# Four graph layers on one core: SyncE's transfers ordered by the framework instead of by the written plan

## The chip, the cores and the metric

The kernel runs on one core of a Trainium2 chip. The metric is device time in microseconds (us). The kernel before took 3899.66 us, the median of three runs (3894.99 to 3900.15). The profile shown here is of one further execution, which took 3905.45 us and has a span of 3903.3 us.

## The reference

The input is 64 graphs of 256 nodes with 512 features each, a 256x256 adjacency matrix for each graph, and the weights of four layers. All is float32. Every layer has the same frame, and the four layers differ in what they do with the normalised features:

```python
h = jnp.maximum(_layernorm(x, axis=-1), 0.0)
x = x + _L0_gnn_ref(h, adj, L0_gnn_W_qk, L0_gnn_W_v)      # scores q k^T * adj, summed, softmax over nodes, times v
...
x = x + _L1_gnn_ref(h, adj, ...)                          # 8 heads, leaky relu of e_i + e_j, masked softmax, times feats
...
x = x + _L2_gnn_ref(h, adj, ...)                          # 8 heads, tanh(adj * Xc Xp^T) times Xp
...
x = x + _L3_gnn_ref(h, adj, nodemask, L3_gnn_Wqk, L3_gnn_Wv)  # q * (adj @ k), softmax over nodes, times v
```

The graphs are independent of each other. Within a graph the four layers follow each other.

## The kernel before

One graph is one chain of 140 named steps (the function `graph`, from L621). Its tiles are 128 partitions (half of the nodes) by 512 features. About five graphs are in work at a time, each in another layer, so that TensorE always finds matmuls of some graph.

**The plan.** Every step has a due time, written out by hand in a table: `TIMES` for the graphs in the middle, which repeat with `PERIOD` = 60.2, and the tables `FIRST` and `LAST` for the graphs at the two ends. `Plan.sequence` (L364) sorts the steps of all graphs by these times, and `Plan.run` (L372) traces them in that order. After each step, `run` ties every new instruction to the one traced before it on the same engine, for the engines listed in `PINNED` (L35). Those engines therefore execute in the order of the due times. The framework, Tile, adds the semaphores, and for an engine that is not tied it chooses the order itself, from its own estimate of when each instruction can start.

**Buffers.** `keep` (L439) makes each kind of buffer once, in a fixed number: five `xt` (a graph's features), three `adj`, two `blocks`, five `at`, two `hn`, three `ht`, two `sq`, three `all`, eight PSUM banks. A step takes the buffer that has been free longest and gives it back with `done`; this bookkeeping happens in the order of tracing, so who gets which buffer is fixed by the plan and does not depend on the order of an engine.

**The transfers.** All 2,747 transfers are issued by SyncE (SP in the profile). For each graph of the steady middle they are, by step:

- `load` (L627): the features `xt` (L629), the adjacency matrix `adj` (L630), and the same matrix once more in 32-wide `blocks`, as four transfers of 64 KB (L634). VectorE turns `blocks` into the transposed matrix `at` (L639); GpSimd turns `adj` into an additive mask in place (L644).
- `sw0` to `sw3`, `swx`, `swy` (L700): VectorE transposes 32x32 squares into `sq`, and this writes them (512 KB) to DRAM as `sq_d`.
- `ht0` to `ht3`, `xpt` (L618): `sq_d` is read back in four transfers, which completes the transpose; TensorE multiplies with `ht` at L607 and with `xpt` at L994. `yr` (L1076) does the same for layer 2's output, and GpSimd and VectorE add it to `xt` at L1083.
- In layer 1: `er` (L835) writes the heads' scores to DRAM, `enes` reads them back to all partitions in two transfers of 1 MB (L839 for the neighbours' scores, L840 for a node's own). VectorE takes the masked maximum of them at L852, then `mr` (L884) writes the maxima and `mb` (L888) reads them back to all partitions, 1 MB. VectorE subtracts them at L910 (step `eb`), ScalarE takes the exponential at L916 (`ex`), and TensorE multiplies at L928 (`po`).
- `store` (L1134): the finished `xt` to the output.

The weights are loaded in the same way among the first graphs' steps (L488 to L560).

Tile gives these transfers eight semaphores in turn, and a transfer waits on SP's queue until the one that had its semaphore before has landed, besides waiting for what it reads and for its buffer.

Of the kernel before, what the change touches and what calls it, by code (L numbers as in the profile page):

```python
# [18 lines left out]
KC = D // P  # L19
# [12 lines left out]
NEG_BIG = -1e10  # L32
BIG = 3.0e38

PINNED = (mybir.EngineType.PE, mybir.EngineType.Activation, mybir.EngineType.DVE, mybir.EngineType.Pool, mybir.EngineType.SP,)  # L35

PERIOD = 60.2
TIMES = {
# [312 lines left out]
class Plan:  # L351
# [20 lines left out]
    def run(self, weights, graph, count):  # L372
        graphs = {-1: weights()}
        for _, b, name in self.sequence(count):
# [5 lines left out]
            for i in traced[n:]:  # L380
                if i.engine in PINNED:
                    if i.engine in self.last:
# [5 lines left out]
class Graph:  # L388
# [5 lines left out]
    def step(self, name):  # L394
        def add(run):
            self.steps[name] = run
            return run
        return add
# [19 lines left out]
def tile_four_gnn_layers(ctx: ExitStack, tc: tile.TileContext, x, adj, nodemask,  # L418
# [5 lines left out]
    nc = tc.nc  # L424
# [14 lines left out]
    def keep(kind, count, shape, pool=None):  # L439

        plan.pools[kind] = [(pool or held).tile(shape, F32, name=f"{kind}{i}") for i in range(count)]
# [35 lines left out]
    def weights():  # L477

        g = Graph(plan)
        step = g.step  # L480
        st = {}


        def plain(name, t, src):
            @step(name)
            def _():
                for r in range(4):
                    nc.sync.dma_start(t[r::4], src.rearrange("(k r d) e -> r d k e", k=KC, r=4)[r])  # L488

        def by_heads(name, k, t, src):  # L490
            @step(f"{name}{k}")
            def _():
                for r in range(4):
                    first = k * P + r * S
                    nc.sync.dma_start(t[r::4].rearrange("p (h u) -> p h u", h=H),
                                        src[:, first:first + S, :].rearrange("h d u -> d h u"))

        def to_all(name, t, src):
            @step(name)
            def _():  # L500
                nc.sync.dma_start(t, src.rearrange("h u -> (h u)").partition_broadcast(P))
        plain("wqk", wqk0_s, wqk0)
        plain("wv0", wv0_s, wv0)
        plain("wv3", wv3_s, wv3)
        for k in range(KC):
            by_heads("w1", k, w1_s[:, k, E:], w1)
            by_heads("w2", k, w2_s[:, k], w2)
        to_all("b1", b1_bc, b1)
        to_all("b2", b2_bc, b2)


        @step("c2")
        def _():
            for s in range(2):
                half = slice(s * U, (s + 1) * U)
                nc.sync.dma_start(c2_s[half, :, half], c2t.rearrange("(a s) k j -> s k a j", s=2)[s])


        @step("wa")
        def _():  # L520
            st["a"] = once.tile([P, 2, D], F32, name="a_bc", bufs=1)
            for s, a in enumerate((a_self, a_neigh)):
                nc.sync.dma_start(st["a"][:, s], a.rearrange("h u -> (h u)").partition_broadcast(P))

        def times_a(k):
            @step(f"sa{k}")
            def _():
                for s in range(2):
                    prod = once.tile([P, D], F32, name="prod", bufs=1)
                    nc.vector.tensor_mul(prod, w1_s[:, k, E:], st["a"][:, s])  # L530
                    nc.vector.tensor_reduce(w1_s[:, k, s * H:(s + 1) * H], prod.rearrange("p (h u) -> p h u", h=H),
                                            AX.X, OP.add)
        for k in range(KC):
            times_a(k)


        @step("mk")
        def _():
            st["mask"] = once.tile([B, N], F32, name="mask_rows", bufs=1)
            nc.sync.dma_start(st["mask"], nodemask)  # L540

        @step("mkp")
        def _():
            pm = g.take("bank", name="mask")
            for c in range(NC):
                nc.tensor.transpose(pm[:, c * B:(c + 1) * B], st["mask"][:, c * P:(c + 1) * P], ident[:B, :B])

        @step("mkv")
        def _():
            nc.vector.tensor_copy(mask_c, g["mask"][:, :NC * B].rearrange("p (c b) -> p c b", c=NC))  # L550
            g.done("mask")


        def part_of_m(e):
            @step(f"wn{e}")
            def _():
                st[f"wn{e}"] = w_n = once.tile([P, 2, KC, P], F32, name="w_n")
                for s in range(2):
                    first = s * D + e * P
                    nc.sync.dma_start(w_n[:, s], wqk3[:, first:first + P].rearrange("(k p) e -> p k e", p=P))  # L560

            @step(f"mt{e}")
            def _():
                for s in range(2):
                    pt = g.take("bank", name=f"wt{s}")
                    for k in range(KC):
                        nc.tensor.transpose(pt[:, k * P:(k + 1) * P], st[f"wn{e}"][:, s, k], ident)

            @step(f"mv{e}")
            def _():  # L570
                st["w_t"] = w_t = once.tile([P, 2, D], F32, name="w_t", bufs=1)
                nc.vector.tensor_copy(w_t[:, 0, :].rearrange("p (k d r) -> p k d r", k=KC, r=4),
                                      g["wt0"].rearrange("p (k r d) -> p k d r", k=KC, r=4))
                nc.vector.tensor_copy(w_t[:, 1, :], g["wt1"])
                g.done("wt0")
                g.done("wt1")

            @step(f"mm{e}")
            def _():
                for k in range(KC):  # L580
                    pm = g[f"m{k}"] if e else g.take("bank", name=f"m{k}")
                    nc.tensor.matmul(pm, st["w_t"][:, 0, k * P:(k + 1) * P], st["w_t"][:, 1, :],
                                     start=(e == 0), stop=(e == KC - 1))
        for e in range(KC):
            part_of_m(e)

        @step("ma")
        def _():
            for k in range(KC):
                nc.scalar.activation(m3_s[:, k, :], g[f"m{k}"], AF.Copy, scale=1.0 / math.sqrt(D))  # L590
                g.done(f"m{k}")


        @step("room")
        def _():
            setup.close()
            late = ctx.enter_context(tc.tile_pool(name="late", bufs=1, side="right"))
            keep("xp", 2, [P, NC, D], late)
            keep("xpt", 2, [P, HP, N], late)
            keep("xc", 1, [P, HP, N], late)  # L600
        return g
# [567 lines left out]
```

## Time and profile before

| What | Value |
|---|---|
| Median of the three runs | 3899.66 us |
| Span of the profiled execution | 3903.3 us |
| TensorE matmuls (PE) | 3811.1 us busy, 98% of the span, 17,474 instructions |
| TensorE weight loads (PEld) | 2375.3 us busy, 61% |
| VectorE (DVE) | 3033.7 us busy, 78% |
| ScalarE (ACT) | 1704.9 us busy, 44% |
| GpSimd (POOL) | 1264.8 us busy, 32% |
| DMA | 717.62 MB, mean 184 GB/s; SP's queue 74.7% of 16 engines' span |

PE and PEld are two rows of one engine: weight loads overlap the matmuls. SP has no busy time in the table, because issuing a transfer does not count as busy. In the timeline of SP each row is an issue: its start is the moment at which everything it waits for has come, and its length is the time that SP was held by the issue itself, not by the transfer. The profile has no landing times for the transfers. When one landed is seen only where some engine waited for it.

### The profile page before, as it was taken

What the parts mean: (1) busy time and instruction counts of PE and PEld (TensorE: products, weight loads), DVE (VectorE), ACT (ScalarE), POOL (GpSimd) and SP (SyncE); (2) the same over time, 40 slices, a digit from 0 to 9 for tenths busy, and PEclk for the clock granted to TensorE, in tenths of its full rate; (3) what the DMA queues carried; (4) which work ended last, traced back from release to release, by engine and by line L of the source; (5) the groups of instructions that cost most, each with busy time, mean ns of one, the idle gap of its engine ahead of it and who ended that gap; (6) DMA issues with size and microseconds to landing.
All of it is one profiled execution on the core that took longest, in us unless ns stands there. A gap on an engine that the chain in (4) does not pass through costs nothing.

```text
span 3903.3 us, 53632 instructions
## 1 busy us (share of the span) xinstructions
PE 3811.1 (98%) x17474; PEld 2375.3 (61%) x17474; DVE 3033.7 (78%) x7641; ACT 1704.9 (44%) x3333; POOL 1264.8 (32%) x1098
## 2 busy tenths in 40 slices
PE   7999999999999999999999999999999999999989
PEld 4756566566566666666666666666566665665564
DVE  6887778777877877877777788788788778777774
ACT  2444444444444444444444444444444444444342
POOL 1332323323323323323323333333233233233231
PEclk9999999999999999999999999999999999999989
DMA  8666777777777788777777877777778777777754
GB/s 211 174 189 172 179 194 174 196 193 179 194 189 184 194 185 189 192 185 181 190 186 186 196 182 187 191 181 191 191 176 200 187 181 192 187 179 193 172 145 107
DMA packets 1657607, 717.62 MB, mean 184 GB/s; under 512 B 1493936, under 2 KB 1549296, under 8 KB 1632752
## 3 DMA queue, kind: packets, MB, share of 16 engines
q1 hardware_dynamic: 1657328, 714.19, 74.7%
q8 instruction: 140, 2.29, 0.3%
q14 instruction: 139, 1.14, 0.1%
HBM read 477.56 MB, written 236.45 MB: 183 GB/s over the span
## 4 chain that ended last, share of the span: by engine, by line
PE 74%; DVE 7%; DMA 4%; SPq 2%; issue 1%; POOL 1%; ACT 1%; DVEq 0%; POOLq 0%; ACTq 0%
PE bank L607 44%; PE bank L928 10%; PE bank L1016 6%; PE bank L1030 5%; PE bank L1102 5%; PE bank L994 3%; DVE junk L852 2%; DVE sq L613 1%; DMA hn<-sq_d 1%; SPq L618 1%; DMA ht<-sq_d 1%; DVE shift L673 1%; PE bank L768 1%; PE bank L718 1%; DVE stats L657 1%
## 5 line engine op out<-in xcount | busy, mean ns | idle before, releaser
L607 PE MATMUL bank<-w_s,ht 128*128 128x256 f32 (+2 forms) x3072 | 963.4, 464 | 30.6 <-DMA ht<-sq_d 24.5
L607 PE MATMUL bank<-wv_s,ht 128*128 128x512 f32 x2048 | 914.4, 594 | 0.1
L607 PEld LDWEIGHTS bank<-w_s,ht 128*128 128x128 f32 x3072 | 572.9, 192 | 364.4 <-issue 215.6
L607 PEld LDWEIGHTS bank<-wv_s,ht 128*128 128x128 f32 x2048 | 380.8, 191 | 426.2 <-issue 410.8
L904 POOL TENSOR_TENSOR pair<-pair,negt 128x1024 f32<-128x1024 f32 x256 | 600.5, 2367 | 50.6 <-ACT pair L897 46.4
L680 ACT ACTIVATE hn<-xt,shift,rstd 128x512 f32<-128x512 f32 x512 | 388.7, 806 | 448.6 <-DVE shift L673 430.3
L928 PEld LDWEIGHTS bank<-feats,pair 128*128 128x128 f32 x4096 | 485.0, 194 | 47.9 <-issue 25.5
L897 ACT ACTIVATE pair<-all,ec 128x256 f32<-128x256 f32 x1024 | 417.2, 494 | 200.1 <-DMA all<-er_d 196.3
L928 PE MATMUL bank<-feats,pair 128*128 128x65 f32 x4096 | 480.8, 276 | 10.2 <-ACT pair L916 10.2
L1055 ACT ACTIVATE pair<-pair 128x512 f32<-128x512 f32 x512 | 294.8, 623 | 420.6 <-DVE pair L1048 420.2
L852 DVE CUSTOM_DVE_ANT_0 junk<-all,adj 128x256 f32<-128x256 f32 x1024 | 444.0, 434 | 35.2 <-DMA all<-er_d 2.1
L607 PE MATMUL bank<-m_s,ht 128*128 128x512 f32 x1024 | 465.9, 599 | 1.3 <-DVE pair L1048 0.8
L668 POOL TENSOR_TENSOR rstd<-rstd,power 128x2 f32<-128x2 f32 x256 | 180.6, 706 | 813.4 <-DVE rstd L664 804.9
L1048 DVE TENSOR_TENSOR pair<-bank,at 128x512 f32<-128x512 f32 x512 | 327.4, 683 | 107.7 <-PE bank L1016 107.0
L1083 POOL TENSOR_TENSOR xt<-xt,hn 128x512 f32<-128x512 f32 x64 | 111.5, 1742 | 924.6 <-DMA hn<-sq_d 657.9
L613 DVE STREAM_TRANSPOSE sq<-hn 128x512 f32<-128x512 f32 x512 | 337.7, 690 | 58.9 <-ACT hn L680 58.9
L657 DVE BATCH_NORM_STATS2 stats<-xt 128x6 f32<-128x512 f32 x512 | 327.2, 680 | 36.4 <-POOL xt L1083 28.6
L910 DVE TENSOR_TENSOR pair<-pair,all 128x1024 f32<-128x1024 f32 x256 | 325.9, 1292 | 9.9 <-DMA all<-m_d 7.5
L607 PEld LDWEIGHTS bank<-m_s,ht 128*128 128x128 f32 x1024 | 189.2, 190 | 213.5 <-issue 207.1
L953 POOL TENSOR_TENSOR xt<-xt,o 128x256 f32<-128x256 f32 x256 | 181.2, 729 | 386.6 <-DVE rs L941 225.1
L916 ACT ACTIVATE pair<-pair 128x1024 f32<-128x1024 f32 x256 | 262.2, 1047 | 45.1 <-DVE pair L910 39.6
L1016 PE MATMUL bank<-xc,xpt 64*128 64x256 f32 x2048 | 255.8, 389 | 1.8 <-ACT xc L1002 1.0
(77 smaller groups left out, 3866.9 us busy)
## 6 DMA issues: line engine op xcount, KB each, us to landing
sq_d<-sq SPq DMA_DIRECT2D x384, 512.0 KB
ht<-sq_d SPq DMA_DIRECT2D x1024, 128.0 KB
all<-er_d SPq DMA_DIRECT2D x128, 1024.0 KB
all<-m_d SPq DMA_DIRECT2D x64, 1024.0 KB
xt<-in_x_dram SPq DMA_DIRECT2D x64, 512.0 KB
xpt<-sq_d SPq DMA_DIRECT2D x256, 128.0 KB
hn<-sq_d SPq DMA_DIRECT2D x256, 128.0 KB
out_dram<-xt SPq DMA_DIRECT2D x64, 512.0 KB
```

Of the source, the lines that this page charges most:

```text
L607: nc.tensor.matmul(p, ht[:, k, c * P:(c + 1) * P], w[:, k], start=(k == 0), stop=(k == KC - 1))
L613: nc.vector.transpose(sq.rearrange("p (r k c i) -> p c k r i", r=4, k=KC, c=NC)[:, c], t[:, c])
L657: nc.vector.bn_stats(stats[:, c, :], g["xt"][:, c, :])
L680: nc.scalar.activation(hn[:, c, :], g["xt"][:, c, :], AF.Relu, bias=st["shift"][:, c:c + 1], scale=st["rstd"][:, c:c + 1])
L852: nc.vector.tensor_tensor_reduce(junk, g["en"][:, h, :], g["adj"][:, c, :], 1.0, -BIG, OP.add, OP.max, st["mx"][:, c, h:h + 1])
L897: nc.scalar.activation(e[:, s, j, :], g["es"][:, h, :], AF.Prelu, bias=st["ec"][:, j, H + h:H + h + 1], alpha=0.2)
L904: nc.gpsimd.tensor_tensor(e, e, g["negt"][:, None].to_broadcast([P, 2, NC, N]), OP.add)
L910: nc.vector.tensor_tensor(e, e, g["m"][:, 2 * p:2 * p + 2, None, :].to_broadcast([P, 2, NC, N]), OP.subtract)
L928: nc.tensor.matmul(po[:, h % 4, :], e[:, s, j, i * P:(i + 1) * P], feats[:, j, h, :], start=(j == 0), stop=(j == NC - 1))
L1016: nc.tensor.matmul(ps[s][:, m, :], g["xpt"][half, p, m * P:(m + 1) * P], g["xc"][half, p, :], start=True, stop=True)
L1048: nc.vector.tensor_tensor(th[:, s], g[f"ps{p}{s}"].rearrange("p (m n) -> p m n", m=NC), g["at"], OP.mult)
L1055: nc.scalar.activation(g[f"th{p}"][:, s], g[f"th{p}"][:, s], AF.Tanh)
```

## The change

`PINNED` loses SyncE. PE, ScalarE, VectorE and GpSimd stay tied to the order of the due times; SyncE's instructions are no longer tied to each other, and Tile orders them. The second part gives the four passes that transpose the last layer's weights (`part_of_m`, once per `e`) separate names for their banks in the plan's bookkeeping. It changes no instruction.

```diff
-PINNED = (mybir.EngineType.PE, mybir.EngineType.Activation, mybir.EngineType.DVE, mybir.EngineType.Pool, mybir.EngineType.SP,)
+PINNED = (mybir.EngineType.PE, mybir.EngineType.Activation, mybir.EngineType.DVE, mybir.EngineType.Pool,)
...
-                    pt = g.take("bank", name=f"wt{s}")
+                    pt = g.take("bank", name=f"wt{s}{e}")
...
-                                      g["wt0"].rearrange("p (k r d) -> p k d r", k=KC, r=4))
-                nc.vector.tensor_copy(w_t[:, 1, :], g["wt1"])
-                g.done("wt0")
-                g.done("wt1")
+                                      g[f"wt0{e}"].rearrange("p (k r d) -> p k d r", k=KC, r=4))
+                nc.vector.tensor_copy(w_t[:, 1, :], g[f"wt1{e}"])
+                g.done(f"wt0{e}")
+                g.done(f"wt1{e}")
```

Set side by side, the instruction lists of PE, DVE, ACT and POOL of the two programs are the same, row by row. The lists of SP hold the same 2,747 transfers in another order. In the steady middle, with b the graph being loaded, the two orders of one period are:

```
before: ... x(b) adj(b) blocks(b) 1-4, er, sw2, en, es, swy, ht2, sw0, yr, ht0, mr,
        mb, swx, sw3, xpt, ht3, sw1, store, ht1, x(b+1) ...
after:  ... x(b), er, sw2, en, es, swy, ht2, sw0, yr, ht0, mr, adj(b+2) blocks(b+2) 1,
        mb, swx, sw3, blocks(b+2) 2, xpt, ht3, blocks(b+2) 3-4, sw1, store, ht1, x(b+1) ...
```

Among the first eleven and the last six graphs more transfers change places.

## The prediction, made before the changed kernel ran

> **What bounds the kernel now.** I read the page's busy table first, then the busy times by stage, then the waits of PE by stage, and last the timeline of SP where the change moves transfers. The page:
>
> ```profile
> PE 3811.1 (98%) x17474; PEld 2375.3 (61%) x17474; DVE 3033.7 (78%) x7641; ACT 1704.9 (44%) x3333; POOL 1264.8 (32%) x1098
> ```
>
> The stages: for each stretch, busy us of PE, PEld, DVE, ACT and POOL (instructions in brackets), the granted clock, the DMA engines' share and GB/s:
>
> ```profile
> 0.00:250.00 250.00, 212.48 (x947) 140.58 (x947) 189.05 (x471) 93.67 (x184) 74.11 (x71) 0.95 0.76 196
> 250.00:500.00 250.00, 241.15 (x1112) 147.10 (x1111) 189.16 (x470) 108.69 (x210) 81.29 (x71) 0.99 0.69 173
> 500.00:3500.00 3000.00, 2980.50 (x13788) 1861.92 (x13787) 2380.90 (x6043) 1348.82 (x2645) 1001.39 (x863) 1.00 0.77 188
> 3500.00:3903.00 403.00, 377.01 (x1634) 225.74 (x1633) 274.56 (x659) 153.72 (x297) 107.96 (x94) 0.97 0.62 153
> ```
>
> PE sets the pace. Outside its matmuls the span holds 92 us: 37.5 in the first 250 us, 8.9 in the next 250, 19.5 in the 3,000 us of the steady middle, 26 at the end. The change touches no instruction of PE, so it can only shrink or widen these gaps. In the middle, PE's waits (us in total, times, longest) are:
>
> ```profile
> PE bank L607 <- DMA ht<-sq_d: 10.1, 11, 1.7
> PE bank L607 <- DVE mx L867: 4.0, 5, 1.0
> PE bank L718 <- DVE junk L776: 3.9, 9, 0.6
> ```
>
> Only the first is a wait for a transfer, so SP's order could win 10 us there and no more.
>
> [...] So whatever stands behind a waiting transfer on SP waits too. The trace agrees: `mr` and `mb` below start 2.49 us apart though the issue of `mr` lasts 0.30. [...]
>
> **The steady middle: cost about 0.** Per graph the change moves five issues, `adj` and four of `blocks`, while `x` stays: 0.47 us for `adj` and 0.63 for each of `blocks` (the medians of the answers on L630 and L634), 3.0 us of SP in all. They leave the place after `x`, and go into three holes of this timeline (start, length, issue):
>
> ```profile
> 1937.89 3.24 SPq L618 DMA_DIRECT2D ht<-sq_d  x4
> 1941.44 0.30 SPq L884 DMA_DIRECT2D m_d<-mr  x1
> 1943.93 0.35 SPq L888 DMA_DIRECT2D all<-m_d  x1
> 1950.90 1.50 SPq L700 DMA_DIRECT2D sq_d<-sq  x2
> 1953.58 2.88 SPq L618 DMA_DIRECT2D xpt<-sq_d  x4
> 1956.56 3.22 SPq L618 DMA_DIRECT2D ht<-sq_d  x4
> 1963.78 0.33 SPq L700 DMA_DIRECT2D sq_d<-sq  x1
> ```
>
> Hole 1, between `mr` and `mb`, is 2.19 us of waiting for `mr` to land; `adj` and one of `blocks` need 1.10. Hole 2, between `sw3` and `xpt`, is 1.18 us; one of `blocks` needs 0.63. Hole 3, between `ht3` and `sw1`, is 4.0 us; two need 1.26. So SP issues everything else when it did. None of the moved loads waits for a buffer there: `adj`(b+2) takes the buffer of the graph whose `mr` has just gone, `blocks`(b+2) one whose transpose is done.
>
> On the wire, the nearest price is the stretch 1910.8 to 1916.0, in which `x`, `adj` and `blocks`, 1 MB, took 5.2 us; `adj` and one of `blocks`, 320 KB, is then 1.6 us, a further one 0.3 (an estimate by bytes)[...]. Behind hole 1 stands `mb`: issued at 1943.93, its first reader L910 started at 1952.37 without a wait, while the DMA engines were at 5% from 1948.0 on. It has some 4 us to spare, and in the whole middle DVE waits for `mb` nowhere. Behind hole 3 stand `sw1` and `ht1`; the DMA share is 0.01 at 1962 to 1963 and 0.00 in the next us, so the two blocks land in idle time. What the loads leave is no gain: after `x` the next work is `er`, at 1921.96, and the DMA share from 1916.0 to 1921.9 is 0.12. DVE waits for `blocks` 1.2 us in the whole run, POOL for `adj` 8.8, both at the start. Bounds: -3 us (some of the `ht` waits), +10 (0.2 us per graph through `mb` or `xpt` in graphs with less room). I take 0.
>
> **The first 250 us: cost about 5.5.** Here the new order differs in what waits. Two places matter.
>
> A and B, layer 1's `ht` of the third and fifth graph. SP before:
>
> ```profile
> 115.72 2.73 SPq L618 DMA_DIRECT2D ht<-sq_d  x4
> 118.56 0.64 SPq L884 DMA_DIRECT2D m_d<-mr  x1
> 121.89 0.34 SPq L700 DMA_DIRECT2D sq_d<-sq  x1
> ```
>
> The new order puts `mr` and that `sq_d` write ahead of the four reads. The write waits for DVE's transposes until 121.89 (SP had been free since 119.2), so the reads are issued from 122.3, the last at 124.3. The nearest landing seen is that of `yr`: last issue near 1936.5, its reader released at 1940.96, 4.4 us. PE wants this `ht` at 125.99, without a gap; it would get it near 128.5: 2.5 us. At B an `adj` load for the sixth graph stands ahead of `ht`, and waits for the buffer that DVE's L852 frees at 154.3; `ht`'s last issue goes from 153.2 to 157.6, landing near 162, against PE at 158.89 plus the 2.5: 0.5 more. Between 150 and 226 PE has gaps of 0.65, 0.74, 1.22, 0.61 and 3.32 us behind DVE, ACT and DMA, which swallow lateness as far as those engines are not late themselves. Bounds 0 and 3; I take 1.
>
> C, the two 1 MB reads of the fifth graph's scores. Before:
>
> ```profile
> 223.41 0.33 SPq L700 DMA_DIRECT2D sq_d<-sq  x1
> 225.94 0.30 SPq L884 DMA_DIRECT2D m_d<-mr  x1
> 226.35 1.75 SPq L1076 DMA_DIRECT2D hn<-sq_d  x4
> 228.20 0.38 SPq L888 DMA_DIRECT2D all<-m_d  x1
> 228.67 0.38 SPq L700 DMA_DIRECT2D sq_d<-sq  x1
> 229.10 0.42 SPq L839 DMA_DIRECT2D all<-er_d  x1
> 229.57 0.76 SPq L840 DMA_DIRECT2D all<-er_d  x1
> ```
>
> The new order issues the L839 read ahead of the write at 223.41, as its buffer is free when L852 ends at 222.23, and the L840 read ahead of `yr` (`hn<-sq_d`). From 226 to 237 the DMA engines moved 230 GB/s, so each MB is about 4.5 us on the wire. The first uses mostly idle wire (0.38 share from 216 to 226), the second goes straight in front of `yr` and `mb`. Both have readers that waited already: DVE L1083 waited 1.24 us for `yr` and L910 1.69 for `mb` (at 236.96), then PE L928 waited 0.89 for the exponential behind it, at 240.43. So the delay reaches PE in full: 4.5 for one MB, up to 8 with both, near 0 if the wire keeps up. Nothing is given back: from 250 to 280 PE is busy 29.97 of 30 us. I take 4.5.
>
> **The end: 0.5.** `mb` of the 61st graph, issued at 3606.12, now stands behind a `swx` that waited until 3608.05; its reader L910 waited for it (2.95 us, until 3614.18), and PE L928 follows at 3617.53. Against that, `ht0` of the last graph may go up to 4 us earlier, but PE came to it at 3714.62 busy. Bounds -1 and 2.
>
> **Sum.** 0 + 1 + 4.5 + 0.5 = 6 us on the span of 3903.3. This span lies 3.6 us above the timed runs' median of 3899.66, within their scatter of 5 us; applied to the median the sum gives 3905.7.
>
> **The rivals.**
> 1. Slower, by a steady loss. `adj` and a block ahead of `mb` take the wire when `mb` is wanted; if their 1.6 us[...] passed the room of `mb`, DVE would stall in order, and the `ht` transposes behind it come late for PE. It decides from the point where the push exceeds the room (4 us in the graph shown). At 0.3 us for each of 58 graphs: 17 us more, 3923. Against it: DVE idles 22% and never waits for `mb` in the middle. Chance 0.22; with it goes the upper part of the start's bounds (C at 8 or more), chance 0.15: 3909 to 3912.
> 2. Faster. The loads leave the neighbourhood of `ht1`, and PE's 10.1 us of waits for `ht` in the middle and 5.4 from 250 to 500 vanish: 3905.7 - 15.5 = 3890. Against it: the loads were issued after `ht1`, not before, and have landed before the next `ht2` and `ht0`. Chance 0.08.
> 3. The order differs but nobody feels it, since gaps at the start swallow A to C: 3899.7. Chance 0.15.
>
> The likeliest, the sum, has 0.40. A measurement of this kernel can tell about 0.2% (7.8 us) from no change: same is 3891.9 to 3907.5. The sum and rival 3 lie in it (0.55), rival 2 below (0.08), rival 1 with the start's upper part above (0.37). The range runs from 3896 (below rival 3 by the scatter) to 3919 (most of rival 1): it leaves out rival 2 and the far end of rival 1.
>
> **What would show it.** SP's timeline around `mr` should show `adj` and a block in hole 1, and `mb` as long after `mr` as before. PE in 500 to 3500 should be busy 2980 us with 19 to 22 us idle; L910 should not gain waits for `mb`; if it gains over 10 us, rival 1 is right. Near 126 PE should wait some 2 us for `ht`, near 240 L928 5 us for L916, with L1083 and L910 late by 4 to 8 us; if not, C is wrong. A shorter wait of PE L607 for `ht` in the middle would speak for rival 2.

## The result, and the profile after

The changed kernel takes 3924.39 us (median of 4 runs, 3919.47 to 3926.46), the kernel before 3897.71 (4 runs): ratio 1.0067, 95% interval 1.0049 to 1.0084. Beside the experiments both ran again on another chip: 3926.66 (5 runs) against 3898.91 (17 runs), ratio 1.0080, 1.0066 to 1.0094. The change costs 27 us, in place of the 6 that were forecast.

The page of the changed kernel's profiled run (3919.47 us, the shortest of its four; the profiled run of before, 3905.45, was longer than the timed ones, so the two traces lie only 14 us apart) has this busy row:

```profile
PE 3818.6 (97%) x17474; PEld 2383.7 (61%) x17474; DVE 3028.8 (77%) x7641; ACT 1705.0 (44%) x3333; POOL 1264.8 (32%) x1098
```

PE has the same 17,474 matmuls, and is busy 7.5 us longer. The table by stage (busy us of PE, PEld, DVE, ACT, POOL, then granted clock, DMA share, GB/s) says where:

```profile
0.00:250.00 250.00, 204.73 (x878) 134.11 (x879) 176.55 (x444) 87.33 (x174) 73.21 (x69) 0.93 0.78 196
250.00:500.00 250.00, 237.96 (x1081) 145.85 (x1079) 184.04 (x468) 108.36 (x210) 77.85 (x66) 0.98 0.67 167
500.00:3500.00 3000.00, 2983.18 (x13828) 1865.63 (x13827) 2379.83 (x6049) 1348.00 (x2639) 999.46 (x866) 1.00 0.78 188
3500.00:3917.00 417.00, 392.73 (x1693) 238.14 (x1691) 288.35 (x683) 161.32 (x311) 114.25 (x98) 0.97 0.62 153
```

In the first 250 us PE got through 878 matmuls where it had done 947, at clock 0.93 for 0.95; in the next 250 it did 1,081 for 1,112. The steady middle is as good as before: 2983 us busy of 3,000 for 2980.5. PE's waits there (us in total, times, longest) add up to no more than they did:

```profile
PE bank L607 <- DVE mx L867: 8.3, 8, 1.4
PE bank L607 <- DMA ht<-sq_d: 4.5, 7, 1.3
PE bank L718 <- DVE junk L776: 2.5, 8, 0.7
```

The timeline of SP in the middle (start, length, issue) shows the moved loads in the three holes:

```profile
1956.36 0.28 SPq L884 DMA_DIRECT2D m_d<-mr  x1
1956.75 0.41 SPq L630 DMA_DIRECT2D adj<-in_adj_dram  x1
1957.21 0.64 SPq L634 DMA_DIRECT2D blocks<-in_adj_dram  x1
1958.64 0.34 SPq L888 DMA_DIRECT2D all<-m_d  x1
1965.38 1.50 SPq L700 DMA_DIRECT2D sq_d<-sq  x2
1966.94 0.62 SPq L634 DMA_DIRECT2D blocks<-in_adj_dram  x1
1968.06 2.83 SPq L618 DMA_DIRECT2D xpt<-sq_d  x4
1971.00 3.49 SPq L618 DMA_DIRECT2D ht<-sq_d  x4
1974.53 1.50 SPq L634 DMA_DIRECT2D blocks<-in_adj_dram  x2
```

`mb` follows `mr` by 2.28 us (2.49 before; over 51 graphs of the middle the medians are 2.55 and 2.50): `adj` and a block cost it nothing. The start is another matter. The same timeline at A (the third graph's `ht1`), B (the fifth's) and C (the fifth graph's 1 MB score reads):

```profile
110.43 0.68 SPq L884 DMA_DIRECT2D m_d<-mr  x1
119.44 0.34 SPq L700 DMA_DIRECT2D sq_d<-sq  x1
119.88 3.14 SPq L618 DMA_DIRECT2D ht<-sq_d  x4
...
156.22 0.39 SPq L630 DMA_DIRECT2D adj<-in_adj_dram  x1
156.66 0.63 SPq L634 DMA_DIRECT2D blocks<-in_adj_dram  x1
157.40 3.07 SPq L618 DMA_DIRECT2D ht<-sq_d  x4
...
226.26 0.33 SPq L839 DMA_DIRECT2D all<-er_d  x1
227.41 0.33 SPq L700 DMA_DIRECT2D sq_d<-sq  x1
230.16 0.29 SPq L884 DMA_DIRECT2D m_d<-mr  x1
230.50 0.34 SPq L840 DMA_DIRECT2D all<-er_d  x1
233.44 1.75 SPq L1076 DMA_DIRECT2D hn<-sq_d  x4
```

At A, SP issued nothing for 8.3 us: at its head stood the write of the fourth graph's squares, which DVE had not finished, and behind it the four reads of `ht`. PE's timeline then has five waits that are new or longer than before (in brackets at the end of a row: the idle time before it, and what ended it):

```profile
126.14 4.22 PE L607 MATMUL bank<-w_s,ht 128*128 128x272 f32 x10 [4.43 <-DMA ht<-sq_d]
163.43 6.86 PE L607 MATMUL bank<-w_s,ht 128*128 128x272 f32 x22 [2.53 <-DMA ht<-sq_d]
246.04 0.47 PE L718 MATMUL bank<-ident,wc 128*128 128x128 f32 x1 [4.56 <-DVE bank L1123]
372.26 3.64 PE L994 MATMUL bank<-xpt,c_s 128*128 128x256 f32 x8 [1.81 <-DMA xpt<-sq_d]
415.22 6.05 PE L607 MATMUL bank<-w_s,ht 128*128 128x512 f32 x8 [4.38 <-DMA ht<-sq_d]
```

The first three are A, B and C (at C, DVE is late with L1123 because it stands in L1083, where it waits 6.5 us for `yr`). The last two lie in the stretch that the prediction had not costed; call them D (`xpt`) and E (`ht2` of the sixth graph, where the kernel before waits 2.35 us). What I had not looked for comes behind each of them. The windows right after the five waits (columns as in the table by stage):

```profile
126.00:130.00 4.00, 3.86 (x10) 2.95 (x11) 0.18 (x2) 0.00 (x0) 0.00 (x0) 0.57 1.13 266
164.00:168.00 4.00, 4.00 (x12) 3.09 (x11) 2.16 (x8) 0.00 (x0) 1.49 (x2) 0.57 0.99 295
246.00:250.00 4.00, 3.96 (x7) 1.84 (x8) 3.89 (x7) 2.40 (x5) 1.88 (x3) 0.58 0.93 130
372.00:376.00 4.00, 3.74 (x11) 3.11 (x12) 0.16 (x1) 0.65 (x2) 0.70 (x1) 0.57 1.02 131
413.00:420.00 7.00, 4.78 (x6) 2.19 (x7) 3.55 (x15) 4.33 (x11) 1.36 (x1) 0.51 0.93 223
```

The same windows of the kernel before, at A and at B:

```profile
126.00:130.00 4.00, 4.00 (x20) 3.35 (x20) 2.50 (x10) 0.70 (x1) 1.98 (x2) 1.00 1.19 208
164.00:168.00 4.00, 3.26 (x15) 2.55 (x15) 3.48 (x12) 1.52 (x2) 1.39 (x2) 1.00 1.12 241
```

PE is busy and gets little done: 10 to 12 matmuls in 4 us, where before has 20 and 15 (its other three windows are at clock 1.00 too). With each of the five waits the granted clock goes to 0.50, for 3.4 us (from 126.5, 164.0, 245.9 and 372.2 us on) and at E for 6.8 (from 413.2). The same work then takes about twice the time: D's eight matmuls of L994 above take 3.64 us, and the eight from 1961.34 us on in before, at clock 1.00, take 1.95. In the traces every stretch at half clock but the last, which outlasts the program, is a multiple of 3.41 us long (3.4, 6.8, 10.2, 13.7, 17.1), and in each trace they all begin and end on one grid of 3.41 us, to within 0.03. The length of a wait does not settle whether one comes: 1.8 us was enough at D, and 3.3 us at 221.8 in the kernel before was not. In one pair it went with how the wait falls on the grid. PE waits 3.3 us for `mx` at L873 in both kernels; these are the grid's windows (from one of its points to the next) over that wait, one in the changed kernel, then two in before:

```profile
225.47:228.88 3.41, 0.34 (x1) 0.00 (x0) 3.34 (x6) 0.00 (x0) 2.96 (x2) 1.00 0.55 168
220.07:223.49 3.42, 1.75 (x5) 0.44 (x3) 3.42 (x4) 0.00 (x0) 3.42 (x2) 1.00 0.00 0
223.49:226.90 3.41, 1.76 (x6) 0.95 (x7) 3.31 (x7) 1.32 (x3) 0.93 (x1) 1.00 0.39 156
```

In the changed kernel PE was busy for a tenth of one window, and a half-clock stretch follows; in before the wait lay across two windows, each half busy, and none follows. So part of the half clock is chance: the same wait for `mx` brought it in 9 of the 15 traces in which nothing was put into it.

### The profile page after: what moved, and what is told of

It reads as the page before. It is cut to its first block, busy times and chain, and to the rows that moved or that the text cites. A ratio compares the mean times of both kernels' runs of the same rounds, so it can differ in the third digit from the quotient of the medians.

```text
span 3917.7 us, 53534 instructions
## 1 busy us (share of the span) xinstructions
PE 3818.6 (97%) x17474; PEld 2383.7 (61%) x17474; DVE 3028.8 (77%) x7641; ACT 1705.0 (44%) x3333; POOL 1264.8 (32%) x1098
## 4 chain that ended last, share of the span: by engine, by line
PE 75%; DVE 7%; DMA 3%; SPq 2%; issue 1%; POOL 1%; ACT 1%; POOLq 0%; DVEq 0%; ACTq 0%
PE bank L607 44%; PE bank L928 11%; PE bank L1016 6%; PE bank L1102 5%; PE bank L1030 5%; DVE junk L852 3%; PE bank L994 3%; DMA hn<-sq_d 1%; DVE sq L613 1%; DVE shift L673 1%; PE bank L768 1%; DMA all<-er_d 1%; SPq L618 1%; PE bank L718 1%; SPq L1076 1%
## 5 line engine op out<-in xcount | busy, mean ns | idle before, releaser
L928 PEld LDWEIGHTS bank<-feats,pair 128*128 128x128 f32 x4096 | 490.5, 196 | 47.4 <-issue 27.9
L928 PE MATMUL bank<-feats,pair 128*128 128x65 f32 x4096 | 485.8, 278 | 10.0 <-ACT pair L916 10.0
L1083 POOL TENSOR_TENSOR xt<-xt,hn 128x512 f32<-128x512 f32 x64 | 110.9, 1733 | 928.3 <-DMA hn<-sq_d 695.2
```

What stands on the lines that cost most here:

```text
L928: nc.tensor.matmul(po[:, h % 4, :], e[:, s, j, i * P:(i + 1) * P], feats[:, j, h, :], start=(j == 0), stop=(j == NC - 1))
```

## The experiments

**Start or steady?** The first pair ties SyncE in one part of the program only.

```diff
-        for _, b, name in self.sequence(count):
+        for at, b, name in self.sequence(count):
...
+                if i.engine == mybir.EngineType.SP and at < 560:    # e2_free_start: at >= 560
+                    if i.engine in self.last:
+                        self.tc.add_manual_dep(i, self.last[i.engine], mybir.DependencyInfo(
+                            mybir.DependencyClass.NoSync, mybir.DependencyReason.DATA), reason="plan")
+                    self.last[i.engine] = i.name
```

> SyncE tied to the order of the times for all steps due before 560 us (graph 9's loads included), left to the framework from there on, the end included. Theory 'the start': the loss is made before 420 us, so this run equals the kernel before: 3898 us, ratio 0.998 to 1.002, PE busy in 0 to 250 us about 212 us, no half-clock stretch near 126 or 246 us. Rival 'a steady loss' (adj and blocks push mb): it keeps nearly the whole loss, 3917 to 3924 us. Rival 'the end': it keeps the part that the end makes, a few us, 3902 to 3906.

> The mirror image: left to the framework before 560 us, tied after it. Theory 'the start': the whole loss stays, 3917 to 3926 us, with PE waits of 4 us near 126 and 246 us and 2 to 4 us near 163, 372 and 415 us, each followed by a half-clock stretch. Rival 'a steady loss': 3898 to 3905 us. The two runs' losses should add up to that of the change.

Tied start: 3899.89 us, ratio 1.0007 (0.9998 to 1.0015). Free start: 3920.11, ratio 1.0062 (1.0049 to 1.0075). The window 120 to 450 us of the first, then of the second:

```profile
120.00:450.00 330.00, 317.20 (x1511) 200.43 (x1510) 260.38 (x644) 146.69 (x279) 110.21 (x95) 1.00 0.71 181
```

```profile
120.00:450.00 330.00, 303.90 (x1384) 190.68 (x1383) 240.42 (x589) 135.49 (x259) 106.76 (x88) 0.95 0.72 174
```

1,384 matmuls for 1,511, clock 0.95 for 1.00. The loss is made at the start; as its cause, a steady loss and a loss at the end fall (up to 5.8 us for the two together is within the interval of the tied start). The two losses, 0.0007 and 0.0062, add up to the 0.0067 and 0.0080 of the change within their intervals.

**The five places.** A tied kernel, whose order of SyncE is that of before with single transfers put ahead of others (each number is graph, step, number in the step, counted from 0):

```diff
+MOVES = ((((1, "mr", 0), (3, "sw0", 0)), (2, "ht1", 0)),          # A
+         (((5, "load", 1), (5, "load", 2)), (4, "ht1", 0)),       # B
+         (((4, "enes", 0),), (1, "swy", 0)),                      # C
+         (((4, "enes", 1),), (1, "yr", 0)),                       # C
+         (((7, "load", 0),), (3, "sw3", 0)),                      # D
+         (((9, "load", 2),), (6, "er", 0)), (((9, "load", 3),), (6, "enes", 0)))   # E
...
+        for what, ahead in MOVES:
+            moved = [e for e in sp if e[0] in what]
+            sp = [e for e in sp if e[0] not in what]
+            at = [e[0] for e in sp].index(ahead)
+            sp[at:at] = moved
+        for (_, p), (_, i) in zip(sp, sp[1:]):
+            self.tc.add_manual_dep(i, p.name, mybir.DependencyInfo(
+                mybir.DependencyClass.NoSync, mybir.DependencyReason.DATA), reason="plan")
```

> The order of the kernel before, tied throughout, with five displacements alone put in, as the framework makes them: A (mr of the second graph and sw0 of the fourth ahead of the third graph's ht1), B (adj and a block of the sixth graph ahead of the fifth's ht1), C (the fifth graph's two 1 MB score reads ahead of swy and of yr of the second), D (x of the eighth ahead of sw3 of the fourth), E (two blocks of the tenth ahead of er and of the first score read of the seventh). Theory 'these five places': it shows most of the loss, +12 to +26 us, 3910 to 3924 us, with the same five PE waits. Rival 'it needs the whole rearrangement' (weights split up, ht1 moved past xpt and so on): under half of it, 3898 to 3908 us.

> The changed kernel itself beside the other three on one chip, for a second trace of it: the profiled pair differs by 14 us and the medians by 27, so either its waits differ from run to run (then this trace shows other or more waits than the first, and a half-clock stretch more for each), or the first trace is typical and the kernel before is the one that varies. Time 3919 to 3927 us either way.

> e6_five again, beside k1_five_fill5: 3915.6 us within 3, all theories alike.

All five: 3915.64, ratio 1.0047 (1.0035 to 1.0060), and in the second set of runs 3921.16, 1.0055 (1.0041 to 1.0068). So nine transfers in the wrong place, of some 2,700, make 18 to 21 of the 27 us. The second trace of the changed kernel (r1_after) has the same five waits (4.45, 2.57, 5.93, 1.64, 4.05 us): they belong to the order, not to the run. From 120 to 450 us PE's lateness against the trace of before grows by 22.4 us in the changed kernel, 22.3 in r1_after and 20.3 in e6_five. Then each alone:

> The order of before with displacement A alone (mr of the second graph and sw0 of the fourth ahead of the third graph's ht1). Theory 'a stall and its clock': PE L607 waits some 4 us for ht near 126 us and then runs 3.4 us at half clock, 6 us together, nothing of it given back: 3905 us. The record's value for A and B together was 1 (bounds 0 to 3): 3900 us. Rival 'swallowed': the gaps that PE has between 150 and 226 us take it up again, so lateness is 6 at 135 us and near 0 at 230: 3899 us.

> Displacement B alone (adj and the first block of the sixth graph ahead of the fifth graph's ht1). Theory: adj waits for its buffer until DVE's L852 and holds ht1 back; PE stalls 2 to 3 us near 159 us with a half-clock stretch of 1.7 us: +3 to 4 us, 3902 us. Rival: B cost something only because A had already made everything late; alone it shows 0.5 us or nothing.

> Displacement C alone (the fifth graph's two 1 MB score reads ahead of swy and of yr of the second graph). The record's value is 4.5 us (bounds 0 to 8): 3903.5 us. Theory now: the wait of PE near 240 us grows by 4 to 5 us and brings one or two half-clock stretches, 6 to 9 us: 3905 to 3908 us. Rival: C was late in the changed kernel only through A and B; alone, with SyncE 5 us ahead, 3 us or less.

> Displacements D and E alone (x of the eighth graph ahead of sw3 of the fourth; two blocks of the tenth ahead of er and of the first score read of the seventh), in the stretch that the record counted as nothing. Theory: 2 to 4 us near 365 us and 3 us near 405 us, half of it half clock: 3904 to 3906 us. Rival: they only became visible behind the late start; alone within 2 us of before.

| places | median us | ratio to before | interval | growth of lateness at the place, us |
|---|---|---|---|---|
| A | 3906.34 | 1.0019 | 1.0011 to 1.0026 | 6.7 |
| B | 3902.02 | 1.0006 | 0.9998 to 1.0014 | 4.3, then 2.1 |
| C | 3908.52 | 1.0024 | 1.0017 to 1.0032 | 7.5 |
| D and E | 3903.29 | 1.0010 | 1.0001 to 1.0019 | 6.1, then 5.2 |

The last column compares the start of the same matmul in the trace of before and in that of the experiment, just ahead of the place and just behind it with its half-clock stretch; a second number is what is left some 10 to 15 us further on. (e1_tied_start, with nothing displaced at the start, moves against before by 1.8 us from 120 to 450 us.) The ratios sum to 0.0059, 23 us, near the 0.0062 of the whole free start. A shows the two parts of its price in the windows from 120 to 130 us of e3_A: 4.4 of the 10 us without work, and clock 0.66.

```profile
120.00:130.00 10.00, 5.60 (x18) 4.34 (x18) 4.18 (x10) 1.52 (x2) 4.43 (x3) 0.66 1.21 226
```

The clock was down from 122.6 to 129.4 us and PE at work from 125.0: 4.4 us at half, 2.2 lost, 6.6 with the wait. The rival that gaps after 150 us swallow A is wrong: its lateness against before is 1.2 us at 140, 1.4 at 175 and 1.3 at 225. For B that rival is half right: of the 4.3 us, 2.2 are gone by 175, in the gaps of 0.74 and 1.22 us that before has at 166 and 171 and e4_B does not, and the changed kernel gets 2.2 us back at the same place. B grows PE's lateness without A too, so it isn't A's shadow; its time alone can't be told from none.

**What C is made of.** One of its two reads moved at a time:

```diff
-MOVES = ((((4, "enes", 0),), (1, "swy", 0)), (((4, "enes", 1),), (1, "yr", 0)))
+MOVES = ((((4, "enes", 0),), (1, "swy", 0)),)    # c1_en;  c2_es: (((4, "enes", 1),), (1, "yr", 0))
```

> Displacement C split, first half: only the first score read (en, 1 MB) ahead of swy. Theory 'the wire': its MB delays the landing of swy by 3 us, and with it yr, mb and PE: +3 to 4 us, with or without a half-clock stretch, 3902 to 3904 us. Rival 'only the one in front of yr matters': 3899 us.

> Displacement C split, second half: only the second score read (es, 1 MB) ahead of yr. Theory 'the wire': one MB, 4.5 us, ahead of yr and mb, +4 to 6 us, 3903 to 3905 us; the two halves add up to the 9 us of e5_C. Rival 'the halves don't add' (one MB is swallowed by the wait that L1083 has anyway): both under 2 us.

c1_en: 3899.03, ratio 1.0004 (0.9995 to 1.0012); c2_es: 3897.53, 1.0007 (0.9999 to 1.0015). The halves don't add up to C's 1.0024. On the wire they do: from the issue of `swy` to the start of L1083, which needs `yr`, before took 7.8 us, c1_en 10.9, c2_es 10.4, and e5_C with both 14.4. That is 3.1, 2.6, and 6.7 together. (`yr` reads what `swy` writes; in c1_en it was issued 6.1 us after `swy`, in before 2.9.) DVE's waits at L1083, first in c1_en, then in e5_C:

```profile
DVE xt L1083 <- DMA hn<-sq_d: 4.4, 1, 4.4
```

```profile
DVE xt L1083 <- DMA hn<-sq_d: 6.2, 1, 6.2
```

Before waited 1.2. PE behind it waits 2.5 us in c1_en and goes on at full clock. In e5_C it waits 4.3 us, 0.9 of which it had before at L928, works 4.8 us at half clock behind that wait and 3.4 us ahead of it (from 224.7 us, behind its wait for `mx`): 4.3 - 0.9 + 2.4 + 1.7 = 7.5, as in the table. The 1.7 are the chance stretch behind `mx`, which C does not make, so 5.8 are C's own. So the last of a transfer's lateness cost most here: what comes first is taken by slack, and what makes the wait longer (4.3 us of PE in e5_C for 2.5 in c1_en) came with the half clock.

**Is the half clock a cost of its own?** Matmuls whose result nobody reads, put into a wait, keep PE at work in it:

```diff
+FILL = {(2, "fa0"): 4}
...
+            for _ in range(FILL.get((b, name), 0)):
+                self.fill(self.pools["bank"][0])
...
+    plan.fill = lambda p: nc.tensor.matmul(p, ident, wv0_s[:, 0], start=True, stop=True)
```

Each is 0.86 us at full clock (two records of 0.43).

> Displacement A as in e3_A, and four matmuls (ident by a weight, 128x512, into the bank that has been free longest, read by nobody) ahead of the third graph's fa0, so that PE works 3.4 us of the 4.4 us in which it waits there for ht. Theory 'the stall costs twice': the half-clock stretch (122.6 to 129.4 us in e3_A) is gone or halved, PE's lateness grows by some 4.5 us over A instead of 6.7, time 3902 to 3904 us against 3906. Rival 'the clock has another cause' (less work in flight, the small operands after it): the stretch stays and the time is 3906 us or, with the matmuls in the way, 3907.

> The kernel before, SyncE tied, with such matmuls ahead of the twelve steps at which PE of before waits 1 us and more (fa0 of graphs 0 and 1, mm3, po0 of 0, mxp of 1 and 3, xp0 of 4, xp1 of 5, softp0 of 8, mxp of 61, po0 and xp0 of 62), 0.9 to 4.3 us each, under the wait that is there. Theory: half of the 20 to 27 us that before loses to half clock (8.5 of them at 100 to 118 us, 13 at 3684 to 3787) comes back, 3885 to 3890 us, which beats both kernels. Rival: the matmuls mostly delay what comes after the wait, or the clock stays down: 3898 to 3904 us.

> The five displacements of e6_five in the same order of SyncE, with the matmuls of f2_fill and more of them in the five waits (four ahead of fa0 of graph 2, two ahead of fa0 of 4, four ahead of softp3 of 0, one ahead of xc of 4, four instead of two ahead of xp1 of 5). Theory 'half of the loss is clock': it lies 5 to 10 us over f2_fill, at 3887 to 3892 us, with hardly a half-clock stretch between 120 and 450 us; the rest is the waits. Rival 'the waits are all of it': 15 to 18 us over f2_fill, 3897 to 3900 us, as e6_five lies over before.

> The changed kernel, SyncE left to the framework, with the same matmuls. Its order of SyncE is not quite that of the changed kernel, since the framework orders again: adj and block of the sixth graph now stand behind ht1, so B should be gone. Theory: 3885 to 3895 us, 30 us under the changed kernel, faster than the kernel before although its order of SyncE is the late one. Rival: 3904 us and more (the 27 us of the change on top of f2_fill).

> e6_five with matmuls in the five displaced waits alone (four ahead of fa0 of graph 2, two ahead of fa0 of 4, four ahead of softp3 of 0, one ahead of xc of 4, four ahead of xp1 of 5). Theory 'the half clock is a cost of its own': 5 to 8 us below e6_five, 3908 to 3911 us. Rival 'the waits end when SyncE and DVE let them, so the half clock is swallowed by the next wait': within 2 us of e6_five, 3914 to 3917 us, though the half-clock stretches between 120 and 420 us are gone.

| kernel | median us | ratio to before | interval |
|---|---|---|---|
| k1_five_fill5: the five places, filled | 3907.23 | 1.0024 | 1.0010 to 1.0037 |
| f1_A_fill: A, filled | 3906.15 | 1.0022 | 1.0014 to 1.0029 |
| f2_fill: before, twelve waits filled | 3881.65 | 0.9960 | 0.9948 to 0.9973 |
| h1_five_fill: five places and all fills | 3903.98 | 1.0015 | 1.0008 to 1.0023 |
| g1_after_fill16: the changed kernel, filled | 3903.54 | 1.0011 | 1.0003 to 1.0018 |

The plainest comparison is k1_five_fill5 with e6_five, which differ in fifteen matmuls that compute nothing: 0.0024 for 0.0047 and 0.0055. More work for PE takes 9 to 12 us off, half of what the five places cost (the intervals of k1_five_fill5 and r2_five stand apart, those of k1_five_fill5 and e6_five just touch). In the traces it is less: from 120 to 450 us PE's lateness grows by 14.2 us in k1_five_fill5 for 20.3 in e6_five, and at C, where PE still waits 2.6 us behind the fill, by as much as without it. The windows of r2_five, e6_five and then of k1_five_fill5:

```profile
120.00:450.00 330.00, 302.11 (x1352) 188.53 (x1350) 238.82 (x580) 132.59 (x255) 103.11 (x85) 0.94 0.69 168
```

```profile
120.00:450.00 330.00, 304.79 (x1408) 192.58 (x1406) 245.36 (x593) 137.78 (x263) 107.67 (x90) 0.96 0.70 173
```

```profile
120.00:450.00 330.00, 315.99 (x1474) 197.56 (x1475) 250.68 (x611) 140.53 (x269) 106.50 (x90) 0.99 0.71 173
```

(Of the 1,474 records, 28 are the fill's. r2_five also had an unlucky 13.7 us at half clock from 179 us on, where nothing was displaced.) f2_fill does the same to waits that before always had: 15 us faster than before, the fastest kernel of the study, with 0.997 granted over its run where before has 0.993. Its five runs lie within 3 us of each other. Not all of this is the filled waits: of the 21 us between its trace and that of before, 7 arise in the steady middle, where it has no fill, and why is open. The changed kernel itself comes down by 23 us with the fills, though the framework then orders SyncE a little differently (B's loads stand behind `ht1`, yet PE waits 4.9 us there).

Three results don't fit. f1_A_fill has no half clock at A (the window from 120 to 130 us below, for 0.66 in e3_A), and PE's lateness there grew by 3.4 us for 6.7, yet its time is that of e3_A:

```profile
120.00:130.00 10.00, 10.00 (x37) 5.94 (x36) 4.81 (x10) 1.52 (x2) 5.60 (x4) 1.00 1.11 235
```

Its trace had 17.1 us of half clock just before A for e3_A's 13.7, which the fill has no part in, and waited longer at E. PE came to A 3.3 us later than in e3_A and had no wait left behind the fill, which may have run past the landing of `ht`. And h1_five_fill lies 22 us over f2_fill, where 5 to 10 were expected: 12 of the 19 us between their traces arise before 475 us, the rest where the two kernels are the same. g1_after_fill16 lies 22 us over f2_fill too, near where its rival put it and not at the 3885 to 3895 us of the theory: with all these waits filled, the late orders still cost some 20 us by the ratios. So the windows show that PE loses time to the half clock, and k1_five_fill5 that filling the five waits wins some back; how much of the 27 us the clock makes is open.

## Why the prediction was wrong

- **The steady middle, 0:** right, and for the reason given: three holes of SP take the loads, 2.28 us from `mr` to `mb`, PE idle 16.8 us of 3,000 for 19.5. Rival 1, which had most of the chance of a loss, put it in the wrong place; 3923 us was near the result for a reason that isn't so.
- **A and B, "I take 1", bounds 0 and 3:** the step that failed most; alone they cost 7.4 and 2.3 us. The working gave A a 2.5 us wait and let later gaps swallow it. The wait was 4.4: `ht` came at 126.1, 2.4 us ahead of the 128.5 worked out, but PE wanted it at 121.7, 4.3 ahead of the 125.99 that I read from before. In part that is the 17.1 us of half clock that before's profiled run had just ahead of it, for 13.7 in the changed kernel's. That one run was taken as the timetable, and it was a late one: the unfilled kernels tied to the same order come to A 2.2 to 5.7 us earlier. Behind the wait came 2.2 us lost to half clock in e3_A, and the gaps gave nothing of A back. B's 0.5 was a wait of 2.4 us and a half-clock stretch, 4.3 together, of which the gaps gave 2.2 back.
- **C, 4.5, bounds 0 and 8:** the mechanism is right, the size off: 9.4 us by the ratio (6.6 to 12.5), 5.8 in the trace. The first MB, called nearly free, cost 3.1 at the reader; the second 2.6, not 4.5; and neither alone reaches PE "in full": in c1_en PE's wait grows by 1.6 us. Together they make 6.7 at the reader, which slack shortens and half clock lengthens. That a MB issued ahead of `swy` and `yr` delays them by its time on the wire was an assumption of the author that no run had shown. c1_en agrees with it: with 1 MB ahead of `swy`, `yr`, which waits for `swy` to land, was issued 6.1 us after it in place of 2.9. PE met the delay at L718, behind DVE's queue, and not at L928 as foretold.
- **From 250 to 500 us, counted as nothing:** D and E cost 3.9 us (0.4 to 7.4). I had looked for displaced transfers only up to 250 us and at the end.
- **The end, 0.5:** e1_tied_start, whose middle and end are free, leaves 2.7 us for both together, at most 5.8 (ratio 1.0007, interval up to 1.0015); nothing there contradicts it.
- **The term that was missing** is the clock: 1.7 us for each 3.4 us that PE works at half (an estimate, half the length, from L994's 3.64 us for 1.95). The five waits of the changed kernel are 17.7 us, 3.2 of them there before; the stretches behind them and behind the wait for `mx` add some 11; gaps that the lateness swallows take some of it back, so that 22.4 are left at 450 us. The prediction read the clock column (0.95, 0.99) and took it as a fact of the stage, when it was a price on most of the long waits (127 of the 145 of 2 us and more that began at full clock, counted below).

## What to carry to other kernels

Of PE's waits of 2 us and more in these traces, 127 of 145 came with a stretch of half clock, and each 3.4 us of work at half lost some 1.7. Where PE sets the pace, price such a wait as the wait plus some 2 us, an estimate from this kernel alone, and look at the granted clock behind every gap. Take the time at which an engine wants something from more than one trace. Compare a new order of transfers with the old one over the whole start, place by place, since the queue that waited at its head cost time here at the start, where buffers and weights are still filling (ratio 1.0062), and not in the steady round (1.0007 with the end). Where a wait can't be removed, work for PE that nobody needs may be worth its place, but has to be measured: here the kernel with 30 such matmuls was 15 us faster, and four at A alone brought nothing.

## What the runs showed of the hardware

The half clock was not expected to matter: half the length of its stretches is 21 us in the trace of e1_tied_start, 27 in that of before, 37 in that of the changed kernel and 11 in that of f2_fill, waits inside them included. By the grid's windows of 3.41 us: the 18 traces have 120 windows at full clock, from 67 us on, in which PE was busy less than 43% of the time, and all were followed by a window at half; of 19,681 in which it was busy 58% and more, 8 were, most of their work L928's; in between, 13 of 82. (In the traces of before and of the changed kernel alone: all 17; 1 of 2,189, at 97.2 us of before; 1 of 9, at D.) By length: of PE's waits begun at full clock, 13 of 222 between 1 and 2 us had a half-clock stretch begin in them or within one window behind, 82 of 100 between 2 and 3.9 us, and all 45 longer ones (in those two traces 1 of 26, 12 of 15, and all 6). What sets the clock is not in the traces; these are counts of what stood beside it.

How the clock came back went with the work. Of the windows at half clock in which PE was busy 90% and more, almost without L928, all 106 were followed by full clock; of those busy over 95% with most of it L928, whose matmuls are small (128x65), all 93 were followed by another half. At half clock 16 of these matmuls took 3.52 us in before (from 110.26 us on), at full clock 32 took 3.68 (from 1957.82). The long stretches at about 100 us and near the end are mostly of that kind; what it is about these matmuls no run separates.

The half clock varies from run to run: in twelve traces of kernels that are alike up to there, the piece at about 100 us is 3.4, 10.2, 13.7 or 17.1 us. That goes with the times of before scattering over 15 us (35 runs) while f2_fill's scatter over 3 (five runs).
